# The output convolution's remaining whole products by quarter blocks: five more of them, in a fused convolution and attention block

## The chip, the cores and the metric

The kernel runs on one core of one Trainium2 chip. Its metric is the device time of one execution in microseconds. Of the kernel before there are three timed runs, with a median of 2210.68 us (2210.54 to 2213.66), and one profiled execution. The engines are called by the profile's short names: PE is TensorE (PEld its weight loads), DVE is VectorE, ACT is ScalarE, POOL is GpSimd, and SP is SyncE, which only issues DMAs here. TensorE's results land in PSUM, of which this kernel makes four slots of two banks: three with the tag "big", one with the tag "av". A bank holds 512 float32 values in each of 128 partitions.

## The reference

Eight images of 512 channels and 32 x 32 places, all float32. Each image goes through a group norm and this block, and is added to its result:

```
t = silu(bn(conv1x1(x, cv1_w)))            # 512 -> 512 channels
ys = [t[:, :256], t[:, 256:]]
for i in range(2):
    z = silu(bn(conv3x3(ys[-1], m_cv1_w[i])))
    z = attention(z, m_qkv_w[i], rw[i] + rh[i])   # 4 heads of 64, over 1024 places
    z = silu(bn(conv1x1(z, m_cv2_w[i])))
    ys.append(ys[-1] + z)
out = x + silu(bn(conv1x1(concat(ys), cv2_w)))    # 1024 -> 512 channels
```

The change is in the last line, called cv2 here: per image a product of a 512 x 1024 matrix of weights with a 1024 x 1024 matrix (channels by places).

## The kernel before

The images go in four pairs; a pair's first image is called a, its second b. In each pair the two images share the 3x3 convolutions, which work on tiles of the image (a Winograd form), while attention and cv2 run for one image after the other. The code is straight-line Python. A scheduler at compile time puts the instructions of each engine into a fixed queue: the order of the code is their priority, an instruction that would not be ready is passed by a later one that is, and `issue_after` ties an instruction behind another on its engine. Slots of SBUF and PSUM are handed out by tag.

cv2 is done by Strassen's method in Winograd's form (function `strassen`): the 2 x 2 blocks of the weights and of the input give seven products of a 256 x 512 block of weights with a 512 x 512 block of input instead of eight. They are called M1 (weights "11"), M2 ("12"), M3 ("s4"), M4 ("22"), M5 ("s1"), M6 ("s2") and M7 ("s3"). The inputs of M4 to M7 are sums of input blocks, called t1 (for M5), t2 (M6), t3 (M7) and t4 (M4), which VectorE adds beforehand; the sums of weights lie in HBM. A whole product is eight float32 matmuls of 128 x 128 weights with 512 columns in `product` (L1350, the matmul is L1356); the profile records each as two. The four output blocks are finished by `finish`: ScalarE applies scale, bias and SiLU into one of four tiles, and the POOL queue adds the input image to it by a DMA that accumulates, then stores it.

Some products are already done by quarters, in `by_quarters` (L1392): the same method once more inside a product, so seven multiplications of quarter blocks, each two matmuls of 256 columns (L1404), where eight would be the plain way. It takes four sums of quarter blocks of the input (`quarter_sums`, L1369, at L1372 to 1375) and four sums of weights, which are loaded ready-made. It takes two half-used PSUM slots: one bank for the running multiplication (called x_), one bank whose two halves hold two others (z_, y_). VectorE takes the results out as they come: five adds of 256 columns (L1410) and one of 512 (L1427). After each multiplication it calls `beside()`, an object of the class `Beside` (L1438), which may issue one "fill", a matmul of a product of other data (at a rate such as (1, 1), every time, or (2, 3), two times in three), and one step of a list of VectorE work.

Who used which before: image b of the first three pairs does M6, M7 and M4 by quarters (`by_quarters3`, L1553), with the 16 matmuls of M2 and M3 as fills. Image a of these pairs does all products whole: `part3` (L1512) adds t2 and t3 (L1517, L1519), then t4 (L1528), issues M2 and M3, then M6, M7 and M4, and finishes the four blocks in the order 0, 1, 2, 3, each as soon as its products are there. It is called by `a3(bottom_a, scaled)()` behind the last small convolution (`m2`) of the pair.

The fourth pair is written out by hand (from about L2640 on), since nothing follows it. There a's M6, M7 and M4 are by quarters, with the matmuls of b's M2 and M3 as fills at every multiplication; b's M6 is by quarters, with the matmuls of b's M7 as fills, and b's M7 (`m7_whole`, L1693) and M4 (`m4_pieces`, L1702, in three pieces) are whole. `c12_early` and `c12_late` (L1676, L1679) add the second output block from M5, M6 and M3.

Between b's `b2()` and `b3(bottom)` the code of the first three pairs also prepares the input tiles of the next pair's convolution (`tiles_steps`, L559, called at L2769). Each step there clears the two edge columns of a tile with two memsets (L591, L592) of 128 x 32 values, on POOL unless the call says otherwise.

Of the kernel before, what the change touches and what calls it, by code (L numbers as in the profile page):

```python
# [32 lines left out]


# [3 lines left out]

# [24 lines left out]
def kernel(  # L63
# [449 lines left out]
    def stages(act, small, ps_big, ps_av, n_pt):  # L513
# [943 lines left out]
        def strassen(b, ws, top, tags, tile_of, l2=None):  # L1457
# [3 lines left out]
            def sums_tile(tag):  # L1461
                return act.tile([P, 2, NM, ROWS, F], F32, tag=tag, name="t_in")
# [49 lines left out]
            def part3(bottom, after=None):  # L1512
                t1 = kept["t1"]
                t2, t3 = sums_tile("k"), tile_of("t3").rearrange("p a c (h w) -> p a c h w", w=F)
                with tc.issue_after(after.ins) if after else nullcontext():
                    for part in range(2):
                        tt(t2[:, part], bottom[1][part], t1[:, part], ALU.subtract)  # L1517
                    for part in range(2):
                        tt(t3[:, part], bottom[1][part], top[1][part], ALU.subtract)  # L1519
                quarters = {}  # L1520
                if l2:
                    for name, t in (("s2", t2), ("s3", t3)):
                        quarters[name] = quarters_of(halves(t), l2.room(name))
                        for _ in quarters[name].steps:
                            pass
                t4 = sums_tile("q")
                for part in range(2):
                    tt(t4[:, part], t2[:, part], bottom[0][part], ALU.subtract)  # L1528
                ps1, ps5, m1, m5 = (kept[k] for k in ("ps1", "ps5", "m1", "m5"))
                w12, s4 = ws("12"), ws("s4")  # L1530
                if l2:
                    return by_quarters3(quarters, bottom, ps1, ps5, m1, m5, w12, s4, t4)
                for part in range(2):
                    product(ps1, w12, bottom[0], [part], onto=True)
                    product(ps5, s4, bottom[1], [part], onto=True)
                finish(0, ps1)

                def new(name, t):
                    ps = ps_big.tile([P, 2, HALF], F32, tag="big", name="c_new")
                    product(ps, ws(name), halves(t))  # L1540
                    return ps

                tt(m1, new("s2", t2), m1, ALU.add)
                c12 = tile_of("o1")
                tt(c12, ps5, m1, ALU.add)
                finish(1, c12)
                tt(m1, new("s3", t3), m1, ALU.add)
                tt(m5, m5, m1, ALU.add)
                finish(2, m5)
                tt(m1, m1, new("22", t4), ALU.subtract)  # L1550
                return lambda: finish(3, m1)

            def by_quarters3(quarters, bottom, ps1, ps5, m1, m5, w12, s4, t4):  # L1553
                ends, u3, c12 = [], tile_of("o2"), tile_of("o1")
# [69 lines left out]
        def rest_apart(ws, kept, bottom, t2, t3, t4, new, finish, l2):  # L1624
# [60 lines left out]
                    tt(c12[0], c12[0], m1, ALU.add)  # L1685
                    finish(1, c12[0])

            def m7(q):
                onto("s3", q)
                tt(m5, m5, m1, ALU.add)  # L1690
                finish(2, m5)

# [528 lines left out]
    for p in range(NP):  # L2221
# [411 lines left out]
        if not more:  # L2633

            def by_rows(t):
                return t.rearrange("p c (h w) -> p c h w", w=F)

            def pt_pair():
                return [by_rows(act.tile([P, NM, HALF], F32, tag="pt", name="t_in", bufs=6)) for _ in range(2)]

            def wide(tag):
                t = act.tile([P, 2, NM, HALF], F32, tag=tag, name="t_in")
                return [by_rows(t[:, part]) for part in range(2)]

            def acc_tile():
                return act.tile([P, 2, HALF], F32, tag="acc", name="c_sum", bufs=2)

            whole = []

            def load_whole(q):  # L2650
                whole.append(ring([P, HW], "x_res"))
                q.dma_start(whole[-1], x[ib, ts(len(whole) - 1, P), :])

            def x_room(name):
                return room_of(*(act.tile([P, 2, 2, HALF // 2], F32, tag="x", name="t_q", bufs=NX) for _ in range(2)))

            l2 = SimpleNamespace(of=l_of, room=x_room)
            for _ in range(2):
                load_whole(nc.sync)
            ts_a = [], [], []  # L2660
            rest_a = s.rest_apart(w_of, heads[ia].kept, bottom_a, *ts_a, acc_tile, s.finish_apart(ia), l2)
            end = s.attention_fast(qkv, z[:, :, 1], at_of(ib, 1), {NG: rest_a.m2_half})
            y3b = act.tile([P, NH, NM, HALF], F32, tag="v", name="y3b")
            end.sums()
            for t, new in zip(ts_a, (wide("k"), pt_pair(), wide("q"))):
                t.extend(new)
            sums_a = s.sums_apart(top, bottom_a, *ts_a)
            rest_a.m2_m3()
            with tc.issue_after(end.evicted.ins):
                last = [next(sums_a) for _ in range(4)][-1]  # L2670
            with tc.issue_after(last.ins):
                end.spread()
            with tc.issue_after(s.inverted[0].ins):
                rest_a.add_m2()
                last = [*sums_a][-1]
            with tc.issue_after(last.ins):
                scaled = end.scale()
            with tc.issue_after(scaled.ins):
                rest_a.add_m3()
                for _ in rest_a.prepare("s2"):  # L2680
                    pass
            last = s.m2(1, z[:, :, 1], Y2[1], lambda oc, half: img(y3b[:, half, oc, :]))
            bottom = [[side(Y2[1], half), img2(y3b[:, half])] for half in range(NH)]
            top = load_tops(ib, Y1[1], "pt", 6)
            ts_b = [], [], []
            cz = act.tile([P, 4, 2, HALF], F32, tag="z", name="cz")
            outs = [cz[:, j, h] for j in (2, 3) for h in range(2)]
            outs += [act.tile([P, HALF], F32, tag="rs", name="c_out", bufs=4) for _ in range(4)]
            outs += [act.tile([P, HALF], F32, tag="h", name="c_out", bufs=2) for _ in range(2)]
            finish, out_of, flush = s.finish_last(ib, whole, lambda: outs.pop(0))  # L2690
            kept_sums = [cz[:, j] for j in range(2)]
            rest_b = s.rest_apart(w_of, heads[ib].kept, bottom, *ts_b, lambda: kept_sums.pop(0), finish, l2)
            fills = []
            rest_b.fills_m2(fills)
            m2_end = fills[-1]
            fills[-1] = lambda: (m2_end(), rest_b.add_m2())
            rest_b.fills_m3(fills)
            q = SimpleNamespace(beside=s.Beside(fills, (1, 1)), banks=s.quarter_banks())
            q = q.banks, q.beside
            for _ in range(2):  # L2700
                fills.pop(0)()
            for _ in rest_a.prepare("s3"):
                pass
            rest_a.m6(q)
            q[1].steps.append(rest_a.prepare("22"))
            for t, new in zip(ts_b, (wide("k"), pt_pair(), wide("q"))):
                t.extend(new)
            sums_b = s.sums_apart(top, bottom, *ts_b)
            q[1].steps.append(islice(sums_b, 4))
            rest_a.m7(q)  # L2710
            q[1].rest()
            q[1].steps.append(rest_b.prepare("s2"))
            for _ in range(2):
                load_whole(nc.gpsimd)
            rest_a.m4(q)
            q[1].rest()
            rest_b.fills_m7(fills)
            q[1].steps.append(sums_b)
            rest_b.m6(q, False)
            q[1].rest()  # L2720
            rest_b.c12_early()
            while fills:
                fills.pop(0)()
            rest_b.c12_late()
            rest_b.m7_whole()
            flush()
            rest_b.m4_pieces(out_of)
            flush()
            continue
        a1, a1_more, a2, a3 = s.strassen(  # L2730
            ia, w_of, top, {"m1": ("p1", 1), "m5": ("p2", 1)}, tile_of
        )
        behind = {NG: a1}
        if p == 0:
# [13 lines left out]
        def room_b(name):  # L2748
# [5 lines left out]

        b1, b1_more, b2, b3 = s.strassen(
            ib, w_of, top, {"m1": ("p3", 1), "m5": ("p4", 1)}, tile_of,
            SimpleNamespace(of=l_of, room=room_b, spare=("p1", "p2"), late=late_outs)
        )
        b1()
        b1_more()  # L2760
# [5 lines left out]
        vs = v_units()  # L2766
        ecs = [{}, {}]
        for g in range(G):
            steps = s.tiles_steps(Y1[g], putter(vs, g), [0, 1], ecs[g])  # L2769
            for _ in range(3):  # L2770
                next(steps)
            with tc.issue_after(s.inverted[0].ins):
                for _ in steps:
                    pass
# [113 lines left out]
```

## Time and profile before

| | |
|---|---|
| median of three runs | 2210.68 us (2210.54 to 2213.66) |
| profiled execution, its own time | 2212.26 us |
| its span, first to last instruction | 2210.8 us |
| mean granted TensorE clock | 0.998 |
| cv2 of the second pair, M2's first row in the chain to the next convolution | 1092.46 to 1171.53 us |
| the same of the third pair, image b's quarter blocks | 1680.00 to 1711.87 us |
| the fourth pair behind its last attention | 2127.35 us to the end |

A line of the profile gives the line of the code, the engine, the operation, what is written from what (`c_q<-t_q,wls` is the bank of a quarter block from a quarter sum and a sum of weights), partitions x elements, and a count; then busy time and mean duration, or, in a timeline, start and length, and in brackets the idle time before it and who ended it. The chain is the work that ended last, followed back from the last instruction; it counts loads and matmuls of TensorE together. A tile's name tells its role: `c` are PSUM slots of M1, M5 and what is added onto them, `c_new` those of whole products, `c_q` those of quarter blocks, `m_kept` the kept M1 and M5, `t_in` sums of blocks, `t_q` sums of quarter blocks, `cz` a shared area for t3 and for sums, `w_rows`, `w_d` and `v_in` belong to the next convolution's tiles. Records of TensorE overlap: the time that one takes in a row of them is the distance of their starts.

### The profile page before, as it was taken

The numbers are of one execution on the slowest core, as the hardware profiler recorded it, in microseconds if no ns is written. First come the engines' busy times: TensorE is split into PE (matmuls) and PEld (weight loads), VectorE is DVE, ScalarE is ACT, GpSimd is POOL, SyncE is SP. The second block draws the span as 40 slices with busy tenths as digits, with TensorE's granted clock in tenths as the row PEclk, the third lists the DMA queues.
The fourth block names the chain that finished last, engine by engine and source line by source line (L and its number), as shares of the span: only waits on it lengthen the run. The fifth ranks groups of instructions, "written<-read, shape, count | busy, mean of one in ns | idle before, by whom it ended". The sixth has DMA issues, their size and how long they took to land.

```text
span 2210.8 us, 40830 instructions
## 1 busy us (share of the span) xinstructions
PE 2181.7 (99%) x16486; PEld 1109.3 (50%) x16486; DVE 1801.0 (81%) x2935; ACT 1094.1 (49%) x1320; POOL 222.9 (10%) x409
## 2 busy tenths in 40 slices
PE   7999999999999999999999999999999999999998
PEld 3653437343484444734458443564345734383445
DVE  8988879878978688976887868997787877897676
ACT  7455553554225666366314676455622465336543
POOL 4322210000210000000012000000002100000001
PEclk9999999999999999999999999999999999999999
DMA  8954447212583324612159141542126801261224
GB/s 271 316 169 134 172 149 261 83 49 78 152 285 95 119 83 129 204 54 73 59 133 328 34 165 37 184 139 78 59 67 171 299 31 44 92 205 38 68 59 116
DMA packets 135528, 291.93 MB, mean 132 GB/s; under 512 B 33732, under 2 KB 61376, under 8 KB 134308
## 3 DMA queue, kind: packets, MB, share of 16 engines
q1 hardware_dynamic: 102708, 201.01, 27.3%
q0 software_dynamic: 32624, 88.23, 13.5%
q8 instruction: 132, 2.16, 0.4%
q14 instruction: 64, 0.52, 0.1%
HBM read 219.58 MB, written 69.60 MB: 131 GB/s over the span
## 4 chain that ended last, share of the span: by engine, by line
PE 91%; DVE 7%; ACT 1%; issue 1%; DMA 0%; POOL 0%; DVEq 0%; ACTq 0%
PE av_ps L1119 19%; PE l_ps L1082 18%; PE c_ps L675 10%; PE c L1356 7%; PE p_ps L958 7%; PE ps L545 5%; PE m_ps L1336 5%; PE x_ps L1776 4%; PE c_q L1404 4%; PE c_new L1356 3%; PE p_ps L964 3%; PE c L1388 2%; PE s_ps L1137 1%; PE c_new L1388 1%; DVE acc L1103 1%
## 5 line engine op out<-in xcount | busy, mean ns | idle before, releaser
L1086 ACT ACTIVATE pt<-l_ps 128x1024 f32<-128x1024 f32 x512 | 495.7, 1023 | 328.1 <-PE l_ps L1082 252.1
L1082 PE MATMUL l_ps<-q,kr 64*64 64x512 f32 x4096 | 485.5, 590 | 0.9 <-ACT pt L1086 0.9
L1119 PE MATMUL av_ps<-pt,vT 64*64 64x512 f32 x4096 | 484.7, 590 | 1.3 <-DVE z L1127 1.1
L1103 DVE TENSOR_TENSOR acc<-acc,pt 128x1024 f32<-128x1024 f32 x362 | 442.6, 1223 | 37.9 <-ACT pt L1086 9.8
L1119 PEld LDWEIGHTS av_ps<-pt,vT 64*64 64x64 f32 x4096 | 156.1, 133 | 280.6 <-issue 234.3
L1082 PEld LDWEIGHTS l_ps<-q,kr 64*64 64x64 f32 x4096 | 157.5, 133 | 270.3 <-issue 246.6
L675 PE MATMUL c_ps<-v_in,u 128*64 128x128 f32 x4320 | 238.5, 273 | 0.0
L675 PEld LDWEIGHTS c_ps<-v_in,u 128*64 128x64 f32 x4320 | 235.8, 137 | 4.9 <-issue 4.7
L1127 DVE TENSOR_TENSOR z<-av_ps,z 128x512 f32<-128x512 f32 x64 | 43.9, 686 | 97.8 <-ACT z L1126 97.7
L1336 PE MATMUL m_ps<-z,m_sb 128*128 128x512 f32 x256 | 114.0, 592 | 0.0
L958 PE MATMUL p_ps<-t_z,sq 128*128 128x512 f32 x224 | 105.9, 595 | 0.0
L680 ACT COPY c_m<-c_ps 128x512 f32<-128x512 f32 x48 | 28.1, 586 | 150.6 <-PE c_ps L675 137.0
L517 ACT ACTIVATE t<-m_ps,bh,sh 128x512 f32<-128x512 f32 x64 | 46.3, 774 | 94.7 <-PE m_ps L1336 93.5
L1100 DVE TENSOR_TENSOR acc<-pt 128x1024 f32<-128x1024 f32 x64 | 78.0, 1219 | 14.2 <-PE s_ps L1137 8.7
L958 PE MATMUL p_ps<-z,sq 128*128 128x512 f32 x168 | 81.3, 604 | 0.8 <-ACT z L517 0.7
L1336 PEld LDWEIGHTS m_ps<-z,m_sb 128*128 128x128 f32 x256 | 47.9, 190 | 56.5 <-issue 51.9
L1195 DVE TENSOR_TENSOR z<-z,rs 128x512 f32<-128x512 f32 x64 | 42.2, 685 | 28.8 <-DMA rs<-r_dram 28.7
L517 ACT ACTIVATE z<-z,bh,sh 128x512 f32<-128x512 f32 x64 | 48.7, 809 | 25.2 <-DVE z L737 25.0
L958 PEld LDWEIGHTS p_ps<-t_z,sq 128*128 128x128 f32 x224 | 39.5, 191 | 36.5 <-issue 34.4
L517 ACT ACTIVATE c_out<-c,bh,sh 128x512 f32<-128x512 f32 x12 | 14.0, 1271 | 85.7 <-PE c L1388 61.7
L1776 PE MATMUL x_ps<-t_x,sw 128*128 128x512 f32 x128 | 55.9, 592 | 0.0
L964 PEld LDWEIGHTS p_ps<-sq,z 128*128 128x128 f32 x336 | 43.5, 191 | 22.0 <-issue 12.8
(408 smaller groups left out, 3298.2 us busy)
## 6 DMA issues: line engine op xcount, KB each, us to landing
u<-u SPq DMA_DIRECT2D x135, 512.0 KB
y_in<-y SPq DMA_DIRECT2D x32, 512.0 KB
rs<-r_dram SPq DMA_DIRECT2D x126, 128.0 KB
sq<-sq SPq DMA_DIRECT2D x42, 384.0 KB
x<-in_x_dram SPq DMA_DIRECT2D x28, 512.0 KB
r_in<-r SPq DMA_DIRECT2D x28, 512.0 KB
c_out<-in_x_dram POOLq DMA_DIRECT2D x56, 256.0 KB, 7.0
out_dram<-c_out POOLq DMA_DIRECT2D x56, 256.0 KB, 3.9
```

What stands on the lines that cost most here:

```text
L517: silued[0] = nc.scalar.activation(dst, src, AF.Silu, scale=sh[:, k : k + 1], bias=bh[:, k : k + 1])
L545: last_product[0] = nc.tensor.matmul(ps[:, half, :], w_of(k), rhs_of(k, half), start=(k == begin), stop=(k == end))
L675: conv_product[0] = nc.tensor.matmul(to[o], us[cp][:, k, row, c, o], rhs, start=(k == 0), stop=(k == NM - 1),)
L958: nc.tensor.matmul(ps[:, o, :], w[:, o, :], rhs, start=not onto, stop=True, skip_group_check=onto)
L964: nc.tensor.matmul(v[:, ts(j, P)], rhs[:, ts(j, P)], w[:, 2, :], start=j == 0 and not onto, stop=True, skip_group_check=True,)
L1082: nc.tensor.matmul(ps[kh * HD : (kh + 1) * HD, hd, :], kr[r, c, o : o + HD], q[r, c, ts(half, HALF)], start=True, stop=True,)
L1086: last_exp[0] = exp = nc.scalar.activation(pt, ps, AF.Exp, scale=SCALE)
L1103: ins = nc.vector.tensor_tensor(accs[g], accs[g], pt[i], ALU.add)
L1119: nc.tensor.matmul(avs[g][hd * HD : (hd + 1) * HD, kh, :], vT[r, j, o : o + HD], pt[i][r, hd, :], start=(j == 0), stop=(j == NJ - 1),)
L1336: nc.tensor.matmul(pss[half][:, oc, :], m2_sb[:, n, k, ts(oc, P)], ao[:, k, ts(half, HALF)], start=(k == 0), stop=(k == NM - 1),)
L1356: nc.tensor.matmul(ps[:, o, :], w[:, k, ts(o, P)], rhs[part][:, c], start=(k == 0 and not onto), stop=(k == KB - 1), skip_group_check=onto,)
L1776: nc.tensor.matmul(ps[:, o, :], w[:, c, ts(o, P)], rhs[c], start=(c == 0 and not onto), stop=(c == 1), skip_group_check=onto,)
```

## The change

Three things change.

Image a of the second and third pair (`p` of 1 and 2; the first pair stays as it was, since the sums of quarter weights are only made there) does M6 and M4 by quarters, in a new function `by_quarters2`. M2's first four matmuls go ahead; the other twelve of M2 and M3 are fills at rate (1, 1) beside M6 and, those that are left, beside M4. t3 and t4 are added in steps beside M6 instead of ahead. M7 stays whole and stands between the two; t4's quarter sums are issued behind it. The block that needs M3 is finished when M3's last fill is there, which is in M4. The quarter sums of M6 lie in the area `cz`, those of M4 in the slot "k".

In the fourth pair b's M7 is by quarters. The fills beside go at rate (1, 2), every second multiplication, and the fills of M7 are gone. b's t3 is added beside a's M6, its t2 beside a's M7, its t4 and the quarter sums of t3 beside b's M6. `c12_early` still comes behind b's M6, `c12_late` behind b's M7.

The edge columns of the next convolution's tiles are cleared by VectorE where `p` is not 0.

```
+            def by_quarters2(x, bottom, ps1, ps5, m1, m5, w12, s4, t3, t4, steps):
+                fills, c12 = [], tile_of("o1")
...
+                for ps, w, rhs, behind in ((ps1, w12, bottom[0], behind_m2), (ps5, s4, bottom[1], behind_m3)):
+                    for part in range(2):
+                        fill_units(fills, ps, w, rhs, [part], True)
+                    fills[-1] = lambda last=fills[-1], behind=behind: (last(), behind())
+                for _ in range(4):
+                    fills.pop(0)()
+                banks = quarter_banks()
+                beside = Beside(fills, (1, 1))
+                beside.steps.append(steps)
+                by_quarters(banks, ws("s2"), l2.of("s2"), x, m1, m1, ALU.add, beside)
+                beside.rest()
+                y = quarters_of(halves(t4), l2.room("22"))
+                m7 = ps_big.tile([P, 2, HALF], F32, tag="big", name="c_new")
+                product(m7, ws("s3"), halves(t3))
+                for _ in y.steps:
+                    pass
+                u3 = tile_of("o2")
+                tt(u3, m7, m1, ALU.add)
+                tt(m5, m5, u3, ALU.add)
+                finish(2, m5)
+                by_quarters(banks, ws("22"), l2.of("22"), y, u3, u3, ALU.subtract, Beside(fills, (1, 1)))
+                while fills:
+                    fills.pop(0)()
+                return lambda: finish(3, u3)
...
-            def m7(q):
+            def m7(q, before=None):
                 onto("s3", q)
+                if before:
+                    while q[1].fills:
+                        q[1].fills.pop(0)()
+                    before()
                 tt(m5, m5, m1, ALU.add)
                 finish(2, m5)
...
+            q = s.quarter_banks(), s.Beside(fills, (1, 2))
...
+            ts_b[1].extend(pt_pair())
+            sums_b = s.sums_apart(top, bottom, *ts_b)
+            q[1].steps.append(islice(sums_b, 2))
             rest_a.m6(q)
-            q[1].steps.append(rest_a.prepare("22"))
-            for t, new in zip(ts_b, (wide("k"), pt_pair(), wide("q"))):
-                t.extend(new)
-            sums_b = s.sums_apart(top, bottom, *ts_b)
-            q[1].steps.append(islice(sums_b, 4))
+            q[1].rest()
+            ts_b[0].extend(wide("k"))
+            q[1].steps.append(chain(rest_a.prepare("22"), islice(sums_b, 2)))
             rest_a.m7(q)
...
-            rest_b.fills_m7(fills)
-            q[1].steps.append(sums_b)
+            ts_b[2].extend(wide("q"))
+            q[1].steps.append(chain(rest_b.prepare("s3"), sums_b))
             rest_b.m6(q, False)
             q[1].rest()
             rest_b.c12_early()
-            while fills:
-                fills.pop(0)()
-            rest_b.c12_late()
-            rest_b.m7_whole()
+            rest_b.m7(q, rest_b.c12_late)
...
-            steps = s.tiles_steps(Y1[g], putter(vs, g), [0, 1], ecs[g])
+            steps = s.tiles_steps(Y1[g], putter(vs, g), [0, 1], ecs[g], clear=nc.vector if p else nc.gpsimd)
```

More of the change, by code (lines that the diff above doesn't have):

```diff
@@ L35 @@
 from contextlib import ExitStack, nullcontext
-from itertools import islice
+from itertools import chain, islice
 from types import SimpleNamespace
@@ L1514, in part3, with more_sums @@
                 t2, t3 = sums_tile("k"), tile_of("t3").rearrange("p a c (h w) -> p a c h w", w=F)
+                t4, few = None, l2 and l2.few
+                def more_sums(which):
+                    if which == 3:
+                        for part in range(2):
+                            yield tt(t3[:, part], bottom[1][part], top[1][part], ALU.subtract)
+                    else:
+                        for part in range(2):
+                            yield tt(t4[:, part], t2[:, part], bottom[0][part], ALU.subtract)
                 with tc.issue_after(after.ins) if after else nullcontext():
@@ L1517, in part3 @@
                         tt(t2[:, part], bottom[1][part], t1[:, part], ALU.subtract)
-                    for part in range(2):
-                        tt(t3[:, part], bottom[1][part], top[1][part], ALU.subtract)
+                    for _ in more_sums(3) if not few else ():
+                        pass
                 quarters = {}
                 if l2:
-                    for name, t in (("s2", t2), ("s3", t3)):
+                    for name, t in (("s2", t2),) if few else (("s2", t2), ("s3", t3)):
                         quarters[name] = quarters_of(halves(t), l2.room(name))
@@ L1526, in part3 @@
                 t4 = sums_tile("q")
-                for part in range(2):
-                    tt(t4[:, part], t2[:, part], bottom[0][part], ALU.subtract)
+                for _ in more_sums(4) if not few else ():
+                    pass
                 ps1, ps5, m1, m5 = (kept[k] for k in ("ps1", "ps5", "m1", "m5"))
                 w12, s4 = ws("12"), ws("s4")
+                if few:
+                    steps = chain(more_sums(3), more_sums(4))
+                    return by_quarters2(quarters["s2"], bottom, ps1, ps5, m1, m5, w12, s4, t3, t4, steps)
                 if l2:
@@ L1551, in part3, with behind_m2, behind_m3 @@
                 return lambda: finish(3, m1)
+            def by_quarters2(x, bottom, ps1, ps5, m1, m5, w12, s4, t3, t4, steps):
+                fills, c12 = [], tile_of("o1")
+                def behind_m2():
+                    finish(0, ps1)
+                def behind_m3():
+                    tt(c12, ps5, m1, ALU.add)
+                    finish(1, c12)
+                for ps, w, rhs, behind in ((ps1, w12, bottom[0], behind_m2), (ps5, s4, bottom[1], behind_m3)):
+                    for part in range(2):
+                        fill_units(fills, ps, w, rhs, [part], True)
[11 more added lines that the diff above has]
+                for _ in y.steps:
+                    pass
+                u3 = tile_of("o2")
[6 more added lines that the diff above has]
+                return lambda: finish(3, u3)
             def by_quarters3(quarters, bottom, ps1, ps5, m1, m5, w12, s4, t4):
@@ L2697 @@
             rest_b.fills_m3(fills)
-            q = SimpleNamespace(beside=s.Beside(fills, (1, 1)), banks=s.quarter_banks())
-            q = q.banks, q.beside
+            q = s.quarter_banks(), s.Beside(fills, (1, 2))
             for _ in range(2):
@@ L2729, with room_a @@
             continue
+        def room_a(name):
+            if name == "22":
+                t = act.tile([P, 4, 2, HALF // 2], F32, tag="k", name="t_q")
+                return [t[:, j] for j in range(4)]
+            return [cz[0][:, 2 + j].rearrange("p (i o q) -> p i o q", i=2, o=2)[:, i] for j in range(2) for i in range(2)]
         a1, a1_more, a2, a3 = s.strassen(
-            ia, w_of, top, {"m1": ("p1", 1), "m5": ("p2", 1)}, tile_of
+            ia, w_of, top, {"m1": ("p1", 1), "m5": ("p2", 1)}, tile_of,
+            None if p == 0 else SimpleNamespace(of=l_of, room=room_a, few=True),
         )
@@ L2756 @@
             ib, w_of, top, {"m1": ("p3", 1), "m5": ("p4", 1)}, tile_of,
-            SimpleNamespace(of=l_of, room=room_b, spare=("p1", "p2"), late=late_outs)
+            SimpleNamespace(of=l_of, room=room_b, spare=("p1", "p2"), late=late_outs, few=False)
         )
```

## The prediction, made before the changed kernel was built

> **What bounds the kernel now.** I read the page's busy times and its chain first, then TensorE's own waits in the stretches that the change touches, then the chain in order of time there.
>
> ```profile
> span 2210.8 us, 40830 instructions
> PE 2181.7 (99%) x16486; PEld 1109.3 (50%) x16486; DVE 1801.0 (81%) x2935; ACT 1094.1 (49%) x1320; POOL 222.9 (10%) x409
> PE 91%; DVE 7%; ACT 1%; issue 1%; DMA 0%; POOL 0%; DVEq 0%; ACTq 0%
> ```
>
> TensorE (PE) is busy nearly all the time and is most of the chain, so time is won by taking work from it, as long as nothing makes it wait instead. For the second pair, the chain in order of time (start, length, what, number of records) runs through the whole output convolution:
>
> ```profile
> 1092.46 12.87 PE c L1356 x30
> 1105.34 20.60 PE c_new L1356 x48
> 1125.94 13.73 PE c L1356 x32
> 1139.67 2.58 PE c L1388 x6
> 1142.25 0.86 PE c_q L1404 x4
> ...
> 1145.69 1.73 PE c_q L1404 x8
> ```
>
> The first row is M2 and M3 of the first image, the second its M6, M7 and M4 as whole products, the third M1 and M5 of the second image; then come the second image's quarter blocks with M2 and M3 in between. There is not one step of another engine between them. TensorE's own waits have no entry from 1062 to 1176 us. From 2124 to the end, over the last pair, there is one, behind the last product:
>
> ```profile
> PE g_ps L2789 <- DVE m_kept L1715: 1.1, 1, 1.1
> ```
>
> So each microsecond of matmul saved in these places is a microsecond of the kernel, and the question is what the finer products make TensorE wait for.
>
> **A product as quarter blocks.** A whole product is 16 matmul records of 512 columns: 20.60 / 48 = 0.429 us apart, 6.87 us. By quarters it is seven multiplications of four records of 256 columns, 28 records. What they cost beside other work, waits included, is in the stretch of the second image, in two pairs:
>
> ```profile
> core 0: us, PE busy (x) PEld busy (x) DVE busy (x) ACT busy (x) POOL busy (x), PEclk, DMA share, GB/s
> 1092.46:1105.34 12.88, 12.88 (x32) 5.71 (x31) 12.88 (x20) 3.79 (x4) 1.89 (x4) 1.00 0.24 83
> 1105.34:1125.94 20.60, 20.60 (x49) 9.12 (x49) 18.95 (x34) 3.56 (x4) 3.81 (x8) 1.00 0.42 89
> 1125.94:1139.67 13.73, 13.73 (x33) 6.08 (x33) 12.44 (x17) 4.71 (x5) 5.35 (x7) 1.00 0.78 192
> 1139.67:1171.53 31.86, 31.86 (x119) 21.76 (x119) 20.71 (x41) 6.13 (x6) 3.21 (x5) 1.00 0.58 176
> 1680.00:1711.87 31.87, 31.87 (x119) 21.77 (x119) 20.72 (x41) 6.13 (x6) 3.22 (x5) 1.00 0.59 176
> ```
>
> The stretch of 31.86 us holds 32 whole records (M2, M3: 13.73 us) and three products by quarters: (31.86 - 13.73) / 3 = 6.04 us each. A product gains 6.87 - 6.04 = 0.83 us on TensorE. The granted clock is 1.00 throughout, so that scale does not move.
>
> The Trainium skill, Perfetto Trace Analysis, Optimizing Tensor Performance, Matmuls, says that larger matmuls are more efficient than smaller ones, which speaks against halving the columns. The rows disagree here: 1.73 / 8 = 0.216 us for 256 columns against 0.429 for 512, half within 1%. By the rule, if it ate all that the eighth saves, the sum would lose its five matmul terms; by the rows it keeps them.
>
> **M6 and M4 of the first image, pairs two and three.** Four products: 4 x 0.83 = 3.3 us less TensorE work. What is new runs on VectorE (DVE). The durations, by groups and by tile:
>
> ```profile
> L1517 DVE TENSOR_TENSOR t_in<-ypad,t_in 128x1024 f32<-128x1024 f32 x6 | 7.3, 1216 | 0.0
> L1372 DVE TENSOR_TENSOR t_q<-t_in 128x512 f32<-128x512 f32 x10 | 6.8, 682 | 0.0
> L1410 DVE TENSOR_TENSOR m_kept<-m_kept,c_q 128x256 f32<-128x256 f32 x35 | 14.4, 417 | 26.0 <-PE c_q L1404 26.0
> L1427 DVE TENSOR_TENSOR m_kept<-m_kept,c_q x7: 686/687/689, 610.6 to 2190.9; 128x512 f32<-128x512 f32 x7
> L1543 DVE TENSOR_TENSOR m_kept<-c_new,m_kept x3: 1214/1215/1220, 573.3 to 1655.1; 128x1024 f32<-128x1024 f32 x3
> ```
>
> Each product adds four quarter sums (4 x 0.68 = 2.7 us) and replaces one add of 1.22 by five of 0.42 and one of 0.69 (2.8): 4.3 us more, 8.6 in a pair. VectorE is nearly full up to 1139.67, but the four stretches from 1092.46 to 1171.53 together leave 79.07 - 64.98 = 14.1 us idle, 11.2 of them in the last. The full part also carries the next convolution's input tiles, which are needed only after 1171.53 and can slip into that idle time. 14.1 - 8.6 less the 1.65 that the stretch shrinks leaves about 4 us. I take the work at nothing for that reason. Gone, it would cost what the quarter sums of the second image come late: at most the 8.6 us in a pair.
>
> Inside M6, each multiplication (0.86) is followed by one of the 16 matmuls of M2 and M3 (0.86, two records): a slot of 1.72 us. VectorE has in it one add (0.42) and, in four slots, one of the moved t3 or t4 sums (1.22): 1.64 in 1.72. It fits, barely; I take 0 for it, between 0 and the rival's price below. M7 stays whole and covers t4's four quarter sums (2.7 in 6.87). M4 starts with the add of u3 and of m5 ahead of its first small add: 2 x 1.22 + 0.42 = 2.9 us, needed when the third multiplication starts, which with two fills between is 4 x 0.86 = 3.4 us later. It fits.
>
> Order of the outputs: M2's finish comes after its eighth fill, the finish of M3 only in M4, behind that of the block of M7. Each issues on the POOL queue two accumulating loads and two stores:
>
> ```profile
> c_out<-in_x_dram POOLq DMA_DIRECT2D x56, 256.0 KB, 7.0
> out_dram<-c_out POOLq DMA_DIRECT2D x56, 256.0 KB, 3.9
> ```
>
> Some 11 us a tile with four tiles, and six of the eight come in the last 10 us, so the last two SiLUs wait for tiles. Nothing on TensorE waits for them: their source u3 is next written in the second image's M7. Cost 0. The quarter weights are asked for some 80 us ahead (SP queue, the last of three in this pair); this moves no load.
>
> ```profile
> 1012.69 0.32 SPq L339 DMA_DIRECT2D wl<-l  x1
> ```
>
> **Tile edges.** From the second pair on, eight memsets a pair move from POOL, where they stood in the same queue as the stores, to VectorE:
>
> ```profile
> L591 DVE MEMSET w_rows<- x6: 85/85/85, 585.1 to 1696.9; 128x32 f32 x6
> 1110.90 0.69 DVE L619 TENSOR_TENSOR w_d<-w_rows 128x512 f32<-128x512 f32 x1 [1.62 <-POOL w_rows L591]
> ```
>
> 8 x 0.085 = 0.7 us are added to VectorE, and a wait of 1.6 us for POOL goes. TensorE sees neither: 0. If they had stayed, the wait would grow with the stores that now crowd together.
>
> **The last image.** TensorE loses 0.83 us with M7 by quarters. Thinner fills (every second multiplication) change the order, not the amount; the last pair's M4 of its first image ran without regular fills already:
>
> ```profile
> 2177.75 5.37 PE c_q L1404 x24
> ```
>
> 24 records in 5.37 us are 0.224 each, against 0.216: 0.2 us lost. The two sums now beside the first M6, and the x_res load on POOL that waits for M3's weights, have the 14 fills and the final 10 us before them; I take 0, at most one 1.22 add.
>
> More lies in the tail. Behind M6's last add the chain is no longer TensorE's:
>
> ```profile
> 2192.64 0.43 DVE m_kept L1410
> ...
> 2193.09 1.24 DVE cz L1676
> ...
> 2194.35 1.24 DVE cz L1679
> ...
> 2204.22 0.43 DVE c_out L1753
> ```
>
> In the timeline, TensorE's last product and what follows it are these:
>
> ```profile
> 2194.15 7.05 PE L1710 MATMUL c_new<-t_in,ws 128*128 128x512 f32 x24
> 2202.90 0.41 DVE L1715 TENSOR_TENSOR m_kept<-m_kept,c_new 128x256 f32<-128x256 f32 x1
> 2203.35 0.84 ACT L517 ACTIVATE c_out<-m_kept,bh,sh 128x256 f32<-128x256 f32 x1 [0.22 <-DVE m_kept L1715]
> ```
>
> VectorE adds c12 in two steps (L1676, L1679), then M7 to m1 and m1 to m5, and ScalarE has seven SiLUs to do; the last add ends at 2204.65. TensorE's last product ends at 2194.15 + 7.05 = 2201.20, and subtraction, SiLU and add (0.41 + 0.84 + 0.43) behind it alone would end at 2202.9. So 1.7 us hang on the chain from M6, not on TensorE. With M7 by quarters, both c12 steps can run in the gaps of M7 (0.42 of work per 0.86), and its block's SiLUs lie some 4 us earlier, beside M7. The chain then starts at M7's last add: up to 1.7 us more. Against that, c12's first step (1.24) now stands between M6's last add and M7's first: 0.43 + 1.24 + 0.42 = 2.1 us, needed at the third multiplication, 1.72 us on. Cost 0.4, unless a matmul of M4 fills it.
>
> **Sum**, against the profiled execution (2212.26 us, span 2210.8): -3.3 - 0.8 - 1.7 + 0.4 = -5.4, so 2206.9. That execution is 1.6 above the median of the runs, 2210.68; on the median it is 2205.3.
>
> **Rivals.** *Tail unmoved:* ScalarE and VectorE end as late behind M7 as before. For it: seven SiLUs and as many last adds stay, in an order fixed before the run. Against: two SiLUs have 4 us more. Gain 3.3 + 0.8 - 0.4 = 3.7: 2207.0.
>
> *VectorE eats the first images' gain:* the 8.6 us more delay the second image's sums by as much as TensorE saved. For it: 31.83 of 33.48 us full before 1125.94. Against: the tiles can slip. Only the last image's 2.1 us remain: 2208.6.
>
> *Slower: VectorE's order stops M6.* If a tile step of the next convolution (1.22) is issued between M6's adds, a slot takes 0.42 + 1.22 + 1.22 = 2.86 against 1.72, and the third multiplication, which adds onto the bank that the first add reads, waits. Seven such slots cost 8.0 us a pair; it decides from 2.7 us a pair, about three wedged steps. Price: 2205.3 + 16.0 = 2221. Against it: the second image's quarter blocks run with such steps beside them and show no wait. The Trainium skill, PSUM — Partial Sum Buffer, Terms, says that TensorE and VectorE may not be on one bank at once; the trace agrees so far as that it shows no wait of this kind in the quarter blocks' stretches.
>
> *Small matmuls gain nothing* (the skill's rule above): only the tail's 1.3 remains, 2209.4.
>
> **How the numbers follow.** Forecast 0.57; tail unmoved 0.18; VectorE eats the gain 0.14; slower 0.09; small matmuls 0.02. A measurement of this kernel tells about 0.2%, 4.4 us. The forecast lies 1.0 beyond that bound; nearly all of its chance, 0.53, is faster, and 0.01 of the second case. Same is 0.37: the rest of the forecast, the second, the third and the fifth. Slower is the fourth, 0.09. The range goes from all terms at their best with another 1.0 for the runs' spread (2210.68 - 5.8 - 1.0 = 2203.9) to just above the third and fifth case, 2210.6.
>
> **What would show it.** Right: the second pair's stretch from M2's start to the next convolution falls by about 1.65 us and TensorE's waits there stay empty; c_q records rise by 5 x 28; VectorE's idle share in the second image's stretch falls; no row waits for POOL's w_rows from the second pair on; at the end the last add follows TensorE's last product by about 1.8 us instead of 3.5. Wrong: waits of c_q for the adds of L1410 or the quarter sums, a first tile of the next convolution that comes late, or L1679's SiLUs still behind M7.

## The result and the profile after

The changed kernel takes 2207.08 us (median of 14 runs, 2205.97 to 2207.93) against 2211.39 for the kernel before on the same chip: a ratio of 0.9979, with a 95% interval of 0.9970 to 0.9987. That is 4.3 us less (2.9 to 6.6), where 5.4 were forecast. The profiled execution took 2206.25 us. Head of the page and its chain, after:

```profile
span 2204.8 us, 40989 instructions
PE 2176.4 (99%) x16546; PEld 1117.9 (51%) x16546; DVE 1817.5 (82%) x2996; ACT 1094.1 (50%) x1320; POOL 220.9 (10%) x393
PE 87%; DVE 8%; DMA 2%; issue 1%; ACT 1%; POOL 0%; SPq 0%; DVEq 0%; ACTq 0%; POOLq 0%
```

TensorE is busy 5.3 us less, VectorE 16.5 us more. But the spans, 2210.8 and 2204.8, differ by 6.0 us, more than the medians do. M1 of the first pair's output convolution is ahead of everything that changed; it begins so in the timeline of before, and then of after:

```profile
529.21 3.27 PE L1356 MATMUL c<-y_in,ws 128*128 128x512 f32 x7
```

```profile
527.22 3.70 PE L1356 MATMUL c<-y_in,ws 128*128 128x512 f32 x8
```

Two of the 6.0 us are this start. In all profiles here it lies between 527.1 and 530.4 us, whatever the kernel. So stretches are compared below, not spans: outside the start and the last microseconds they repeat within some 0.1 us, apart from one kind of wait that is named.

**Second and third pair.** From the second group of m_ps products (the last small convolution behind the attention) to the next 3x3 convolution, the stretch table of before and of after has these rows (length; busy time of PE, PEld, DVE, ACT and POOL; clock, DMA share, GB/s):

```profile
1087.15:1171.46 84.31, 84.31 (x239) 45.03 (x237) 70.22 (x117) 19.57 (x19) 14.20 (x23) 1.00 0.48 132
1627.48:1711.80 84.32, 84.32 (x240) 45.03 (x238) 70.22 (x117) 19.54 (x19) 14.22 (x23) 1.00 0.49 132
```

```profile
1085.18:1167.99 82.81, 82.81 (x263) 49.62 (x262) 77.48 (x140) 19.54 (x19) 13.55 (x19) 1.00 0.51 134
1624.67:1707.49 82.82, 82.82 (x263) 49.62 (x263) 77.48 (x140) 19.55 (x19) 13.40 (x18) 1.00 0.51 134
```

1.50 us less a pair, where 1.65 were forecast, and VectorE fills 77.5 of 82.8 us. From M1 on it is 101.92 us before, and 100.45 and 100.99 after. TensorE's waits that are new behind the first pair are only two:

```profile
PE m_ps L1336 <- DVE z L1195: 0.4, 1, 0.4
PE c_q L1404 <- DVE m_kept L1410: 0.3, 1, 0.3
```

The first lies just ahead of the third pair's stretch: row sums of the attention (`rs`, read by the multiply L1195) that landed late. They come and go between executions: in the thicker-fills run below, whose second and third pair are the changed kernel's, they came in time, and the two pairs take 100.28 and 100.29 us, which is the 1.65 in full. The run of the last pair alone, whose pairs are those of before, has one late landing too (102.20 us). With the pairs changed and these products in the old order, the third pair waits for them in five of seven profiles, with the pairs of before in one of three: too few to settle whether the change makes them more frequent. The second wait is in the last pair.

**The last pair.** From a's M6 to the end of TensorE's last product, before takes 2201.20 - 2151.76 = 49.44 us, after 49.54. M7 by quarters saves 0.83 there, and it is all lost again. The largest wait is at the fourth multiplication of a's M6. Around it, before and then after (timeline; TensorE's rows, then VectorE's):

```profile
2155.20 1.03 PE L1404 MATMUL c_q<-t_q,wls 128*128 128x256 f32 x4
2156.07 1.02 PE L1388 MATMUL c_new<-y3b,ws 128*128 128x512 f32 x2
2156.93 1.03 PE L1404 MATMUL c_q<-t_in,wss 128*128 128x256 f32 x4
...
2154.19 0.41 DVE L1410 TENSOR_TENSOR m_kept<-m_kept,c_q 128x256 f32<-128x256 f32 x1
2154.52 1.22 DVE L1590 TENSOR_TENSOR t_in<-y3b,ypad 128x1024 f32<-128x1024 f32 x1
2155.66 0.41 DVE L1410 TENSOR_TENSOR m_kept<-m_kept,c_q 128x256 f32<-128x256 f32 x1
```

```profile
2150.90 1.03 PE L1404 MATMUL c_q<-t_q,wls 128*128 128x256 f32 x4
2152.18 1.13 PE L1404 MATMUL c_q<-t_in,wss 128*128 128x256 f32 x4 [0.26 <-DVE m_kept L1410]
2153.15 1.03 PE L1404 MATMUL c_q<-t_q,wls 128*128 128x256 f32 x4
...
2150.25 0.41 DVE L1410 TENSOR_TENSOR m_kept<-m_kept,c_q 128x256 f32<-128x256 f32 x1
2150.59 1.21 DVE L1638 TENSOR_TENSOR t_in<-y3b,ypad 128x1024 f32<-128x1024 f32 x1
2151.72 0.74 DVE L1410 TENSOR_TENSOR m_kept<-m_kept,c_q 128x256 f32<-128x256 f32 x2
```

The fourth multiplication would start 0.86 us behind the third, at 2151.76; it starts at 2152.18, and the one behind it 0.97 later instead of 0.86. Its bank is free when the second small add has read it, and that add is queued behind L1638, the second of the sums for b's t3. The change did not put this sum there: before, the same sum (L1590) stood in the same place. What the change took away is the fill between the third and the fourth multiplication, which gave the add 0.86 us more. The others are 0.24 us in b's M7, where the small add at 2189.37 stands behind a last add (L1805: the input image is added to a finished tile), and five of 0.05 to 0.11, the 0.97 among them. Together they come to about 1.1 us; before had 0.2 of them.

How long this wait is depends on the row sums again, as the experiments show: where they land about as early as in the profile of before, the stretch is 49.17 and 49.19 us, and about 0.26 of the 0.83 stay.

**The tail**, TensorE's last product and what follows it (timeline after):

```profile
2190.80 6.19 PE L1762 MATMUL c_new<-t_in,ws 128*128 128x512 f32 x22
2195.89 0.41 DVE L1767 TENSOR_TENSOR m_kept<-m_kept,c_new 128x256 f32<-128x256 f32 x1
2196.77 1.03 DVE L1805 TENSOR_TENSOR c_out<-c_out,x_res 128x512 f32<-128x512 f32 x2 [0.47 <-ACT c_out L517]
2197.71 0.41 DVE L1767 TENSOR_TENSOR m_kept<-m_kept,c_new 128x256 f32<-128x256 f32 x1
2198.16 0.84 ACT L517 ACTIVATE c_out<-m_kept,bh,sh 128x256 f32<-128x256 f32 x1 [0.84 <-DVE m_kept L1767]
2199.03 0.42 DVE L1805 TENSOR_TENSOR c_out<-c_out,x_res 128x256 f32<-128x256 f32 x1 [0.85 <-ACT c_out L517]
```

The last add ends 2.46 us behind TensorE instead of 3.45; 1.8 were forecast. TensorE ends at 2196.99, but the last subtraction starts at 2197.71: two last adds, 1.03 us together, stand ahead of it. From TensorE's end to the end of the span it is 7.8 us instead of 9.6.

### The profile page after: what moved, and what is told of

Its sections match the earlier page's. It is cut to its first block, busy times and chain, and to the rows that moved or that the text cites. A ratio compares the mean times of both kernels' runs of the same rounds, so it can differ in the third digit from the quotient of the medians.

```text
span 2204.8 us, 40989 instructions
## 1 busy us (share of the span) xinstructions
PE 2176.4 (99%) x16546; PEld 1117.9 (51%) x16546; DVE 1817.5 (82%) x2996; ACT 1094.1 (50%) x1320; POOL 220.9 (10%) x393
## 4 chain that ended last, share of the span: by engine, by line
PE 87%; DVE 8%; DMA 2%; issue 1%; ACT 1%; POOL 0%; SPq 0%; DVEq 0%; ACTq 0%; POOLq 0%
PE av_ps L1119 19%; PE l_ps L1082 18%; PE c_ps L675 10%; PE p_ps L958 7%; PE c L1356 5%; PE m_ps L1336 5%; PE c_q L1404 5%; PE x_ps L1828 4%; PE ps L545 3%; PE c L1388 3%; PE p_ps L964 3%; PE c_new L1356 2%; PE s_ps L1137 1%; DMA taps<-in_m_cv_w_dram 1%; DVE acc L1103 1%
## 5 line engine op out<-in xcount | busy, mean ns | idle before, releaser
L1504 POOL DMA_DIRECT2D c_out<-in_x_dram x48 | 43.4, 1041 | 273.6 <-ACT c_out L517 271.9
L1195 DVE TENSOR_TENSOR z<-z,rs 128x512 f32<-128x512 f32 x64 | 42.2, 685 | 30.0 <-DMA rs<-r_dram 29.9
```

## The experiments

All were compared with the kernel before on the same chip. The intervals of the ratios reach some 2 us to either side, and the start alone spreads over 3.3 us, so the verdicts rest on stretches of one profile each.

**The parts apart.** Pairs only, with the last pair and the clearing as before:

```
-            steps = s.tiles_steps(Y1[g], putter(vs, g), [0, 1], ecs[g], clear=nc.vector if p else nc.gpsimd)
+            steps = s.tiles_steps(Y1[g], putter(vs, g), [0, 1], ecs[g])
...
-            q = s.quarter_banks(), s.Beside(fills, (1, 2))
+            q = SimpleNamespace(beside=s.Beside(fills, (1, 1)), banks=s.quarter_banks())
...
```

> Only M6 and M4 of image a in the second and third pair by quarters; the last image and the clearing as before. Theory 1 (each place gives what its matmuls save, less its own waits): 2 x 1.65 = 3.3 us less than before, and in the second and third pair the stretch from M1's first matmul to the next convolution shorter by 1.65 us each (the changed kernel's profile had 1.47 and 0.94, the rest lost to attention's row loads, which came later there). Theory 2 (VectorE eats this gain and the change lives from the last image): 0 to 1 us. If the clearing on POOL is needed (theory 3), TensorE waits for tiles of the next convolution and the gain falls below 2 us.

2209.64 us, ratio 0.9990 (0.9981 to 0.9999): 2.0 less. The stretches of the two pairs are 83.19 and 83.51 us, so 1.12 and 0.81 were gained, not 1.5: less than in the whole change. TensorE waits at two places in M4, the same as in the run of all but the clearing below, and in both runs POOL clears.

Last pair only:

```
-            None if p == 0 else SimpleNamespace(of=l_of, room=room_a, few=True),
+            None,
...
-            steps = s.tiles_steps(Y1[g], putter(vs, g), [0, 1], ecs[g], clear=nc.vector if p else nc.gpsimd)
+            steps = s.tiles_steps(Y1[g], putter(vs, g), [0, 1], ecs[g])
```

> Only M7 of the last image by quarters, with its new order of fills; the pairs and the clearing as before. Theory 1: TensorE gains nothing here (0.83 saved, about 0.9 lost in waits of c_q for small adds), and the end comes 1.0 us nearer to TensorE's last product, some 1 us less than before in all. Theory 2: 3 to 4 us less. The forecast had 2.1 us.

2209.82 us, ratio 0.9991 (0.9982 to 1.0000): 1.8 less. From M6 to TensorE's last product it takes 49.76 us, 0.3 more than before; M6's fourth multiplication comes 0.60 us late here. The last add follows TensorE by 2.47. So all that this part gives in this profile, it gives in the tail.

The clearing alone, the kernel before with this in it:

```
+            steps = s.tiles_steps(Y1[g], putter(vs, g), [0, 1], ecs[g], clear=nc.vector if p else nc.gpsimd)
```

> Only the clearing of tile edges by VectorE from the second pair on. Theories 1 and 2: no difference (within 0.5 us); the wait of L619 for POOL goes from the third pair's and second pair's cv2. Theory 3 (the clearing is worth something by itself): 1 us or more.

2211.26 us, ratio 1.0000 (0.9991 to 1.0009): nothing by itself. Its last pair is that of before, with row sums that landed late, and M6's third multiplication waits 0.24 us for the first small add; from M6 on it takes 49.78 us. So late row sums cost something there without the change too.

All but the clearing:

```
-            steps = s.tiles_steps(Y1[g], putter(vs, g), [0, 1], ecs[g], clear=nc.vector if p else nc.gpsimd)
+            steps = s.tiles_steps(Y1[g], putter(vs, g), [0, 1], ecs[g])
```

> The whole change without the clearing by VectorE. Theory 1: the time of the changed kernel within 0.5 us, 4.3 us less than before; waits of L619 for POOL grow in the profile, since more stores stand in POOL's queue, but TensorE does not see them. Theory 3: slower than the changed kernel by 1 us or more, with TensorE waiting for tiles.

2208.76 us, ratio 0.9987 (0.9978 to 0.9996): 1.7 above the changed kernel, with intervals that overlap. Its stretch table (the third pair has 83.52 too), and two multiplications of the second pair's M4 with the VectorE rows around them:

```profile
1088.17:1171.69 83.52, 83.31 (x263) 49.53 (x262) 77.38 (x136) 19.52 (x19) 14.46 (x23) 1.00 0.50 134
```

```profile
1121.28 1.02 PE L1388 MATMUL c<-y_half,wss 128*128 128x512 f32 x2
1122.45 1.13 PE L1404 MATMUL c_q<-t_q,wl 128*128 128x256 f32 x4
...
1119.64 0.69 DVE L600 SCALAR_TENSOR_TENSOR w_rows<-w_ec 128x512 f32<-128x512 f32 x1
1120.24 0.69 DVE L601 SCALAR_TENSOR_TENSOR w_rows<-w_ec 128x512 f32<-128x512 f32 x1
1120.85 1.22 DVE L1520 TENSOR_TENSOR cz<-ypad,y_in 128x1024 f32<-128x1024 f32 x1
1121.98 0.41 DVE L1410 TENSOR_TENSOR cz<-cz,c_q 128x256 f32<-128x256 f32 x1
```

Alone nothing, but together with the pairs' quarter blocks 0.7 us a pair. VectorE does not wait for POOL in these rows: they follow each other without a gap, and the longer waits of L619 that were expected are in none of the pairs behind the first. What differs is the order. With POOL clearing, an add of b's t3 (L1520) stands in the queue ahead of the small add, and the multiplication that could start at 1122.14 starts at 1122.45. With VectorE clearing that add stands later, at 1129.04, and the same place after reads:

```profile
1116.78 0.65 DVE L600 SCALAR_TENSOR_TENSOR w_rows<-w_ec 128x512 f32<-128x512 f32 x1
1116.82 0.09 DVE L592 MEMSET w_rows<- 128x32 f32 x1
1117.35 0.68 DVE L601 SCALAR_TENSOR_TENSOR w_rows<-w_ec 128x512 f32<-128x512 f32 x1
1117.95 0.41 DVE L1410 TENSOR_TENSOR cz<-cz,c_q 128x256 f32<-128x256 f32 x1
```

**Is it the order?** POOL clears, and L1520 is held behind the last small add of a's M4:

```
-        last_out = b3(bottom)
+        last_out = b3(bottom, m4_end[0] if m4_end else None)
```

(`m4_end` holds the last add of `by_quarters2`; `part3` issues t2 and t3 behind it.)

> The changed kernel with the clearing back on GpSimd (as in the run of all but VectorE's clearing), and the last image's sums of t3 (two adds of 1.22 us) held behind the last small add of the first image's M4. Theory 1 (the clearing was worth 0.7 us a pair by the order it gave to VectorE's queue): the stretch from the second m_ps product to the convolution is 82.8 to 82.9 us as with VectorE's clearing. Rival (the waiting for GpSimd's clears itself costs it): 83.4 to 83.6, as with GpSimd's clearing before.

```profile
1088.04:1171.09 83.05, 82.99 (x264) 49.56 (x263) 77.24 (x136) 19.60 (x19) 14.28 (x23) 1.00 0.50 134
1627.11:1709.92 82.81, 82.81 (x263) 49.51 (x262) 77.00 (x136) 19.54 (x19) 13.96 (x23) 1.00 0.53 135
```

The third pair is back at 82.81, the second at 83.05. Taken from the first quarter multiplication on, which leaves the late row sums out, the pairs are at 75.28 and 75.09 us, between 75.69 with POOL's clearing and 74.98 with VectorE's: 1.0 of 1.4 us come back with POOL still clearing. So the order carries most of it. The rest is at M4's third multiplication, whose small add comes 4.06 us behind M4's start in the second pair here, 3.77 after. With POOL's clearing one more tile step of 0.42 us (L630) stands ahead of that add, so this looks like order too; but no run moves that step alone, and the third pair, with the same order, comes at 3.88 and is 0.04 late. The time, 2207.73 (ratio 0.9980, 0.9970 to 0.9990), fits but decides nothing.

**Does another product still pay?** a's M7 in the second and third pair by quarters too, its 12 fills spread at (2, 3):

```
-                m7 = ps_big.tile([P, 2, HALF], F32, tag="big", name="c_new")
-                product(m7, ws("s3"), halves(t3))
...
-                tt(u3, m7, m1, ALU.add)
+                by_quarters(banks, ws("s3"), l2.of("s3"), quarters["s3"], m1, u3, ALU.add, beside)
```

> The changed kernel with one product more by quarters: the first image's M7 in the second and third pair too (its sums in two x tiles, the sixteen matmuls of M2 and M3 spread at two in three over M6, M7 and M4). Theory 1 (a product by quarters gives the 0.83 us that its matmuls save, less the waits for its own adds): the stretch from the second m_ps product to the next convolution, 82.81 us in both pairs of the changed kernel, falls to 82.0 to 82.2 in each, so 1.2 to 1.7 us in all. Theory 2 (VectorE is full in this stretch, and further products gain nothing): 82.6 to 83.2, with waits of TensorE for small adds of 0.2 to 0.8 us a pair.

The order of the m_ps products and M2's first matmuls is another one here, so the comparison starts at the first quarter multiplication, after and in this run (the third pairs have 74.99 and 74.56):

```profile
1093.01:1167.99 74.98, 74.98 (x245) 46.09 (x243) 69.65 (x130) 16.64 (x15) 13.55 (x19) 1.00 0.56 148
```

```profile
1092.73:1167.30 74.57, 74.57 (x258) 47.97 (x256) 72.56 (x138) 16.92 (x15) 13.80 (x19) 1.00 0.61 163
```

0.41 us a pair instead of 0.83, halfway between the two theories: small gaps of 0.03 to 0.1 us in each pair, 0.4 together, eat the other half. VectorE has 2 us left in 74.6. Against the kernel before the ratio is 0.9980 (0.9970 to 0.9990) at 2207.08 us; timing alone can't tell it from the changed kernel.

**The last pair's wait.** The second sum of b's t3 (L1638 in the rows above) is held behind the third small add of a's M6:

```
+                with tc.issue_after(q[1].put.ins):
+                    last = next(steps)
```

> The changed kernel with one add of 1.21 us moved in VectorE's queue: the last image's second sum of t3 (from y3b), which stands between the first and the second small add of the first image's M6 in the last pair, is held behind the third. Theory 1 (this add is what TensorE waits for in M6): from the start of that M6 to TensorE's last product 49.0 to 49.1 us instead of 49.54, with no wait of 0.4 at its fourth product. Rival (the small adds are late because the adds that make y3b are late, which depends on when the row sums land): the wait stays, at 0.06 to 0.6 us as in the other runs with this stretch, and the stretch at 49.2 to 49.8.

```profile
2153.94 1.03 PE L1404 MATMUL c_q<-t_q,wls 128*128 128x256 f32 x4
2154.81 1.03 PE L1404 MATMUL c_q<-t_in,wss 128*128 128x256 f32 x4
...
2153.04 0.74 DVE L1410 TENSOR_TENSOR m_kept<-m_kept,c_q 128x256 f32<-128x256 f32 x2
2155.01 0.42 DVE L1410 TENSOR_TENSOR m_kept<-m_kept,c_q 128x256 f32<-128x256 f32 x1 [1.23 <-PE c_q L1404]
2155.34 1.22 DVE L1639 TENSOR_TENSOR t_in<-y3b,ypad 128x1024 f32<-128x1024 f32 x1
```

No wait, and 49.00 us instead of 49.54. The rival was half right: without the move, the wait does depend on when the row sums land. The multiply that uses them (L1195) starts so long ahead of M6, and the fourth multiplication comes so late: 6.66 us, 0.06; 6.42, 0.18; 6.16, 0.42 (the changed kernel); 5.94, 0.60; 5.59, 0.61 (the run that holds L1520 back, whose third multiplication is 0.40 late already, and whose stretch of 50.12 us is the longest). With the add moved it started 6.43 ahead, and there was no wait; with 6.42 and the add in its place the stretch is 49.34. So at equal row sums the move is worth 0.34, not 0.54. In the three profiles with the last pair as before, where a fill stands in between, the fourth multiplication does not wait, not even at 5.75 (the clearing-alone run). By these profiles the wait needs all three: late row sums, this add in its place, and no fill to cover it. 2206.75 us, ratio 0.9978 (0.9969 to 0.9987).

**Thicker fills.** Four matmuls of M2 ahead of a's M6 instead of two, and the first piece of b's M4, eight matmuls, between the multiplications of b's M7:

```
-            for _ in range(2):
+            for _ in range(4):
                 fills.pop(0)()
...
             rest_b.c12_early()
+            rest_b.fills_m4(fills)
+            q[1].rate = 1, 1
...
```

> The changed kernel with the last pair's fillers laid out otherwise: four instead of two matmuls of M2 ahead of the first image's M6, and the first piece of the last image's M4 (eight matmuls that are computed anyway) between the products of its M7. TensorE computes the same. Theory 1 (the last stretch's 0.8 us were lost because the fillers ran too thin to hide the small adds in M6 and M7): the last stretch, 74.01 us, falls to 73.0 to 73.3. Theory 2 (VectorE has too much to do there, wherever the fillers stand): 73.8 to 74.2, with the waits at other places.

M7 runs without a wait now, M6 loses 0.24 us once, at its third multiplication, and from a's M2 to TensorE's last product it is 73.52 us instead of 74.01 (73.65 in the run below, whose M6 and M7 are the changed kernel's): short of theory 1. But the tail takes it back (timeline of this run):

```profile
2192.95 3.62 PE L1773 MATMUL c_new<-t_in,ws 128*128 128x256 f32 x16
2196.22 0.69 DVE L1816 TENSOR_TENSOR c_out<-c_out,x_res 128x512 f32<-128x512 f32 x1 [0.33 <-ACT c_out L517]
2197.28 0.69 DVE L1816 TENSOR_TENSOR c_out<-c_out,x_res 128x512 f32<-128x512 f32 x1 [0.37 <-ACT c_out L517]
2197.89 0.41 DVE L1778 TENSOR_TENSOR m_kept<-m_kept,c_new 128x256 f32<-128x256 f32 x1
2194.87 4.64 ACT L517 ACTIVATE c_out<-m_kept,bh,sh 128x512 f32<-128x512 f32 x5 [4.31 <-DVE m_kept L1752]
```

Behind M7 there are 3.6 us of matmul left, not 6.2, to cover five SiLUs in a row (4.64); the last add follows TensorE by 3.38 us, nearly as before. 2208.25 us, ratio 0.9985 (0.9976 to 0.9995): no gain.

**The tail.** The last adds behind the last subtraction:

```
-            rest_b.m4_pieces(out_of)
-            flush()
+            last = rest_b.m4_pieces(out_of)
+            with tc.issue_after(last.ins):
+                flush()
```

> The changed kernel with only the last residual adds put behind the last subtraction in VectorE's queue. Theory 1 (the missing 0.7 us of the tail are the two adds of 1.03 us that stand ahead of the last subtraction): the last add ends 1.8 to 2.0 us after TensorE's last product instead of 2.46, the rest as it was: 0.5 to 0.65 us less. Rival (the SiLU or the subtraction's own wait sets it): 2.3 to 2.5. Second rival (the adds that were early now store late, with the last one): 1.8 to 2.0, but 5.8 or more from the last add to the end instead of 5.35, and no gain.

```profile
2197.05 0.42 DVE L1767 TENSOR_TENSOR m_kept<-m_kept,c_new 128x256 f32<-128x256 f32 x1 [0.72 <-PE c_new L1762]
2197.39 1.42 DVE L1806 TENSOR_TENSOR c_out<-c_out,x_res 128x512 f32<-128x512 f32 x3
```

The subtraction starts 0.04 us behind TensorE's end, and the last add follows by 1.80 us, as theory 1 had it. But from there to the end of the span it is 6.6 us, not 5.3, and from TensorE's end 8.4, not 7.8; the time is 2207.71 (ratio 0.9982, 0.9972 to 0.9992). That is the second rival, yet not shown: in seven profiles with the changed kernel's tail the time from TensorE's end to the end of the span lies anywhere from 7.8 to 8.8 us (mean 8.2), in three with the tail of before from 9.4 to 9.6.

**Both edits that took time** (M7 of the pairs and the moved add), put together:

> The changed kernel with both edits that took time from a stretch: the first image's M7 by quarters in the second and third pair, and the moved add in the last. If the stretches add up, the second and third pair take 82.4 us each from their second m_ps product to the convolution (82.8 in the changed kernel), the last pair 49.0 to 49.1 from its M6 to TensorE's last product, and the time is 1.2 to 1.4 us below the changed kernel's: a ratio to the kernel before of 0.9973 to 0.9976. If the moved add brings nothing, 0.8 us below and 0.9976 to 0.9979.

From M1 to the convolution the pairs take 99.89 and 99.91 us, against 100.28 in undisturbed pairs of the changed kernel's code, and the last pair 48.99 from its M6: the stretches add up. 2206.53 us, ratio 0.9975 (0.9965 to 0.9984), the lowest of all, 0.6 below the changed kernel where the stretches say 1.3.

## Why the prediction was right, and where not

The sign, the range and the mechanism of the largest term held; 1.1 us of the forecast's 5.4 are missing. The greater part of the chance, 0.53, was on a gain beyond the 4.4 us that a measurement can tell; 4.3 with its interval does not show one. The terms went apart as follows.

- *M6 and M4 of the pairs, -3.3:* -3.3 where the row sums land in time, -2.4 from M1 on in the profile after. Right in kind and size. M6's slots, 1.64 in 1.72, fit; M4's start, with 2.9 us to do in 3.4, was just late (a gap of 0.04).
- *Tile edges, 0:* this step failed. The memsets are as cheap as said (0.09 us) and no wait for POOL remains behind the first pair, but "TensorE sees neither" is wrong: with POOL's clearing the same quarter blocks lose 0.7 us a pair. The forecast looked for a wait that would grow, and the cost was an order: which add the scheduler puts ahead of the small adds. It is close to the slower rival's mechanism, an add of 1.22 wedged between small ones, but in M4 and not in M6, with a sum of b's t3 and not a tile step, and once a pair and not seven times; the second place of each pair is one tile step of 0.42 more.
- *Last image's M7, -0.8, and the c12 wait, +0.4:* the saving is there, the loss was 0.9. The failed step is "Thinner fills ... I take 0, at most one 1.22 add": 0.5 of the loss is in a's M6, where a fill used to cover an add of 1.21 us that stood there before as well. By the profiles this costs between 0.06 and 0.6 us, with the landing of the row sums, which the forecast did not have; the run with the add moved shows no wait. The other 0.4 are in M7, as much as was priced there, but that is luck: at the place that was priced a matmul of M4 steps in (L1762 at 2185.24), as the forecast allowed, and 0.34 are the wait behind L1805, which it did not see.
- *Tail, -1.7:* -1.8 in the profile after, -1.3 by the means over the profiles with either tail. The chain of c12 did move into M7 (its SiLUs start at 2187.42, beside M7), so the rival of an unmoved tail falls. Of the last add's 1.6 us, 1.0 came; the rest hung on two last adds ahead of the subtraction, which the forecast did not look for, and the run that freed them gained nothing at the end. That the profile meets the forecast is luck: 0.8 of its 1.8 lie behind the last add, where the same tail took from 5.3 to 6.4 us.
- *Small matmuls gain nothing:* falls with the pairs' term. *VectorE eats the first images' gain:* falls too, though the run with M7 shows where it would begin.

## What to carry to other kernels

When products are cut finer, the price of each is set by where its small adds stand in the other engine's fixed queue, not by that engine's busy share: look for every add of a microsecond that could stand between two of them, and pin it behind. A matmul of other data between two multiplications is slack for such an add: before thinning these fills, look what each of them covers. A change that only moves cheap work (here a clearing) can change that order, so ask what the scheduler will put in its place. At a tail, count what must still be done behind the last matmul before moving matmuls forward: they were its cover.

## What the runs showed of the hardware

A wait of TensorE at the start of a multiplication costs about 0.1 us more than itself. In M6's rows above, the four records behind the wait take 1.13 us instead of 1.03, and the next group starts 0.97 us later instead of 0.86. The weight loads (PEld) there:

```profile
2150.72 0.80 PEld L1404 LDWEIGHTS c_q<-t_q,wls 128*128 128x128 f32 x4 [0.49 <-DVE m_kept L1410]
2152.18 0.73 PEld L1404 LDWEIGHTS c_q<-t_in,wss 128*128 128x128 f32 x4 [0.66 <-DVE m_kept L1410]
2152.94 0.84 PEld L1404 LDWEIGHTS c_q<-t_q,wls 128*128 128x128 f32 x4
```

In a run of products the load starts some 0.2 us ahead of its matmul (2150.72 for 2150.90, 2152.94 for 2153.15); at the wait it starts with it, at 2152.18, and by its row it was the load that stood waiting for VectorE, for 0.66 us. The Trainium skill, TensorE: Matmul & The Clock Gate, in its opening table, says that TensorE pulls weight loads ahead of matmuls in flight; the trace agrees for the products without a wait, and shows that the load did not go ahead of the matmul that waited.

Halving the columns of a float32 matmul still costs nothing extra at 99% busy: in the five new products, too, matmuls of 256 columns start 0.216 us apart. And the last microseconds are not a fixed cost: with the same tail, the end came 5.3 to 6.4 us behind the last add.
